# A second Strassen level for three products of the ssm residual, in a conditioned block kernel in float32

## The chip, the cores and the metric

The kernel runs on one core of a Trainium2 chip. The metric is the device time of one execution in microseconds; the median of several runs is given. TensorE (PE in the profile; PEld is its loading of weights) multiplies, VectorE (DVE), ScalarE (ACT) and GpSimd (POOL) work on elements, SyncE (SP) issues most transfers. Each engine takes its instructions in the order in which the program lists them.

## The reference

The reference is one block of a conditioned network over `x` of 2 x 2048 x 512, in float32. With the conditioning row `t` of each of the two batch entries it computes six rows of 512, normalizes, multiplies twice by 512 x 512 weights (the ssm part), and after a second normalization by weights of 512 x 1024 and 1024 x 512 (the ff part). Each part is scaled by a gate and added to `x`:

```python
emb = jnp.dot(jax.nn.silu(t), ada_w) + ada_b
shift_msa, scale_msa, gate_msa, shift_mlp, scale_mlp, gate_mlp = jnp.split(emb, 6, axis=-1)
norm = _ln(x) * (1.0 + scale_msa[:, None]) + shift_msa[:, None]
h = jax.nn.gelu(jnp.dot(norm, ssm_w1) + ssm_b1, approximate=False)
x = x + gate_msa[:, None] * (jnp.dot(h, ssm_w2) + ssm_b2)
norm2 = _ln(x) * (1.0 + scale_mlp[:, None]) + shift_mlp[:, None]
hf = jax.nn.gelu(jnp.dot(norm2, ff_w1) + ff_b1, approximate=True)
x = x + gate_mlp[:, None] * (jnp.dot(hf, ff_w2) + ff_b2)
```

## The kernel before

The 4096 rows are cut into 8 blocks of 512, numbered 0 to 7; blocks 4 to 7 belong to the second batch entry and have other gates. A block passes four stages on TensorE, which the names of the PSUM tiles tell apart: `hA` (hidden of the ssm part), `oA` (residual of the ssm part), `hC` (hidden of the ff part) and `oC` (residual of the ff part). The loop at the end of the kernel interleaves two blocks: with `i` for the block in its ff part, it issues `hC` of block i, `oA` of block i + 1, `oC` of block i and `hA` of block i + 2. Near the end (`ahead`, i = 5) `hA` of block 7 comes before `oC` of block 5, and `oA` of block 7 after it.

Every product is done in Strassen's form. `hA` and `oA` use one level: seven products `P1` to `P7` of half sizes in place of eight, each of eight TensorE records (`group`, the matmul at L475). The operand sums that Strassen needs are made on GpSimd or VectorE (`cut_sum`, L348). `hC` uses a fixed program of 26 products (`products`, L985) whose operand sums `forms` are listed in `HK_B` (20 sums, L923) and whose results are read at L999 (ScalarE) and L1002 (VectorE). `oC` (`residual_in_leaves`) does `P1` and `P6` plainly (L778) and the other five products by a second level: seven rounds, in each of which one leaf of every one of the five products is multiplied (L824), 128 columns wide.

What TensorE sums up in PSUM is added to `x` by VectorE: L739 in `oA`, L789, L838 and L874 in `oC`. In `oA` the result of P1 is not read alone: ScalarE copies it into another bank (L489), on which P2 is added.

PSUM is handed out from two pools: `ps_t` with two banks of the tag `t`, and `ps_g` with two banks for each of the tags `y`, `x` and `v`. A new tile takes the bank of the tile before the last one of its tag, and its first write waits until that tile has been read. The bias rows, already multiplied by the gates, are written into the banks ahead of time (`seed`, L447 and L445).

The order of the work around the matmuls is written out by hand: `hooks` maps a place (a product or a round) to the operations that are issued behind it. So an operation of VectorE that is hooked behind a round stands in VectorE's queue between the reads of that round and the reads of the next.

A normalization (`Norm`) has these steps: `stats` on VectorE (L512, L513); `scales`, eight small instructions on 128 x 4 elements, one of them a power, on GpSimd (L548 to L566); `normal` on ScalarE (L580); `turn`, a transpose in 32 x 32 pieces on VectorE (L591); `move`, 16 transfers that finish the transpose (L600); and `modulate` on ScalarE (L623). Then come the sums for `hA` (`summed`) or the 20 `forms` for `hC`.

The second weights of both parts are multiplied by the gate of the batch entry (`weight_of_second`, L396). This is done again when block 4 begins: `w2` is loaded anew in `oC` of block 2 and multiplied in `hA` of block 4, with the gate row taken into PSUM by `take_gate` (L336); `fw2` follows in `hA` of block 5.

Of the kernel before, what the change touches and what calls it, by code (L numbers as in the profile page):

```python
# [140 lines left out]
def kernel(  # L141
# [97 lines left out]
    ident = const.tile([P, P], F32, tag="ident", name="ident")  # L239
# [20 lines left out]
    b2_bc = work.tile([P, D], F32, tag="gb", name="gb2_0", bufs=2)  # L260
# [39 lines left out]
    def gate_rows_of(g, tag):  # L300
        pa = rows_of(g)
        r = work.tile([P, P] if g == 2 else [P, D], F32, tag=tag, name=f"grows_{g}", bufs=1)
        nc.vector.tensor_tensor(r[:, :P], pa[:, :P], gate_b[g], ALU.add)
        gate_rows[g] = r
# [16 lines left out]
    def store_gates(g):  # L321

        to = gates_dram[g].rearrange("b (n m q) -> m b n q", n=KD, q=G)
        for m in range(P // G):
            rows_m = gate_rows[g][m * G : m * G + B, :P].rearrange("p (n q) -> p n q", n=KD)
            nc.sync.dma_start(out=to[m], in_=rows_m)

    def load_gate(g, b):

        t = work.tile([P, D], F32, tag="g5", name=f"gsb_{g}_{b}", bufs=1)  # L330
        gate_rows[g, b] = load_row(t, gates_dram[g][b])
# [59 lines left out]
    def weight_of_second(w_sb, s, gt, engs, cut=1):  # L391
# [15 lines left out]
        return second_operands(q, s), ops + sums_of_second(q, s, nc.gpsimd, cut)  # L407
# [22 lines left out]

    Q = P // C
# [17 lines left out]
    leaf_row = const.tile([P, 3, P], F32, tag="leaf_row", name="leaf_row")  # L449
    nc.gpsimd.memset(leaf_row, 0.0)  # L450

    def apart_leaves(row, eng):
        a, b = slice(D // 2, D // 2 + P), slice(D // 2 + P, D)
        eng.tensor_tensor(leaf_row[:, 2], row[:, b], row[:, a], ALU.subtract)
# [44 lines left out]
    class Norm:  # L499
# [30 lines left out]
        def squares_on_act(self):  # L530
# [9 lines left out]
            return [lambda: nc.gpsimd.tensor_scalar(less, self.mv[:, :, 0], -1.0, None, ALU.mult)] + [  # L540
# [3 lines left out]
        def scales(self, on_dve=False):  # L544

            n, v = self.name, nc.gpsimd
            ve = small.tile([P, C], F32, tag="ve", name=f"ve{n}")
            v.tensor_scalar(ve, self.mv[:, :, 1], self.of_squares, EPS, ALU.mult, ALU.add)  # L548
            r = small.tile([P, C], F32, tag="r", name=f"r{n}")
            v.tensor_tensor(r, ve, minus_half, ALU.pow)  # L550
            e = small.tile([P, C], F32, tag="e", name=f"e{n}")
            self.rstd = small.tile([P, C], F32, tag="rstd", name=f"rstd{n}")
            self.nmr = small.tile([P, C], F32, tag="nmr", name=f"nmr{n}")
            if on_dve:
                v = nc.vector
                v.tensor_tensor(e, r, ve, ALU.mult)
                v.scalar_tensor_tensor(e, e, -0.5, r, ALU.mult, ALU.mult)
                v.scalar_tensor_tensor(self.rstd, e, 1.5, r, ALU.add, ALU.mult)
                v.scalar_tensor_tensor(self.nmr, self.mv[:, :, 0], -1.0, self.rstd, ALU.mult, ALU.mult)
                return  # L560
            v.tensor_tensor(e, r, r, ALU.mult)
# [4 lines left out]
            v.tensor_scalar(self.nmr, self.nmr, -1.0, None, ALU.mult)  # L566

# [70 lines left out]
        def registers(self):  # L638
# [4 lines left out]
            ]  # L643

# [110 lines left out]

    LEAVES = ("P1", "P2", "P6", "P5", "P7", "P3", "P4")
# [4 lines left out]
    def residual_in_leaves(name, i, hops, wops, leaf_wops, kdim, hooks, last, five, carried):  # L761
# [36 lines left out]
        }  # L798
        seeded = ps["v"].rearrange("p j d -> p (j d)").rearrange("p (n d) -> p n d", d=P)
# [6 lines left out]
        if five:  # L806
            nc.scalar.copy(rooms["P4", "v"][:, :3, :], leaf_row)
# [90 lines left out]
    def gate_bias(g, b, row, name):  # L898

        t = load_row(work.tile([P, D], F32, tag="gb", name=name, bufs=2), row)  # L900
# [14 lines left out]
    def sums_of_registers(program, reg, engs):  # L915


        def op(n, d, f, a, b):
            eng = engs[n % len(engs)]
            if f == "n":  # L920
# [6 lines left out]
    class First:  # L927
# [8 lines left out]
        def summed(self, eng):  # L936
# [3 lines left out]
            return sums_of_first(q, s, eng)  # L940

# [3 lines left out]
    class Second:  # L945
# [77 lines left out]
        def leaf_sums(self, nxt, nx2, five, engs):  # L1023
# [7 lines left out]
            else:  # L1031
                flat = forms.rearrange("p n a r -> p (n a r)")
                r24, r35 = flat[:, : 6 * W], flat[:, 6 * W : (6 + 3 * n35) * W]
                r7 = [flat[:, (12 + n) * W : (13 + n) * W] for n in range(3)]
# [30 lines left out]
    silu = const.tile([P, KD, G], F32, tag="silu", name="silu")  # L1065
# [43 lines left out]
    n1[0].scales(on_dve=True)  # L1109
# [37 lines left out]
    hook(hooks, ("P2",), [lambda: gate_rows_of(2, "grows")] + n1_sums[3:])  # L1147
# [23 lines left out]
    def ff_gate():  # L1171
        take_gate(5, 0)
        found["fw2"] = weight_of_second(fw2_sb, fw2_s, gate[5, 0], (nc.vector,), 4)
# [4 lines left out]
    def gb5_0():  # L1178
        nc.gpsimd.tensor_tensor(gb[5], gate_rows[5, 0], gb[5], ALU.mult)
# [9 lines left out]
    hook(hooks, ("P6",), [lambda: gate_rows_of(5, "g5")])  # L1189
    hook(hooks, ("P6", "P6", "P7", "P7"), [lambda c=c: n2[0].turn(c) for c in range(C)])  # L1190
    hook(hooks, ("P7",), [lambda: n2[0].move((nc.sync,), (0, 1)), lambda: store_gates(5), lambda: load_gate(5, 0)])
    fb2_bc = work.tile([P, D], F32, tag="gb", name="gb5_0", bufs=2)
    load_row(fb2_bc, fb2)
    load_x(2)
    gb[5] = fb2_bc
# [26 lines left out]
    hook(hooks, ("P2",), [n1[2].move, gb5_0])  # L1222
# [3 lines left out]
    hook(hooks, ("P4",), [lambda: store_gates(2)])  # L1226
# [33 lines left out]
    hook(hooks, ("P1",) * 3 + ("P2", "P2", "P6", "P6", "P5", "P5", "P7", "P3"), take(11))  # L1260
# [15 lines left out]

    later, unread_stats = [], []
    for i in range(1, NBLK):
# [7 lines left out]
        if i == 1:  # L1286
# [4 lines left out]
            hook(hooks, (0,), [n1[i + 2].scales])  # L1291
        elif unread_stats:
            hook(hooks, (1, 2, 3, 5, 7), unread_stats)
        if nx2:
            hook(hooks, (3,), [lambda: load_x(i + 1)])
            hook(hooks, (3, 3, 4, 4) if ahead else (1, 2, 3, 4), hA[i + 1].summed(nc.gpsimd))
        elif nxt:
# [196 lines left out]
```

## Time and profile before

| | |
|---|---|
| time, median of 3 runs | 586.76 us (586.58 to 587.15) |
| profiled execution, span | 584.7 us |
| lies around the span, in the median | 2.06 us |
| PE busy | 577.8 us, 99% |
| DVE busy | 416.3 us, 71% |
| POOL busy | 428.2 us, 73% |
| ACT busy | 263.2 us, 45% |

The span runs from the first instruction to the last of one profiled execution. The execution's own time has no record besides its span; the median of the runs shown lies 2.06 us above it. In the rows of a timeline the columns are the start in us, the time taken in us, the engine, the line, the operation, what is written and read, the shapes and the count; in brackets the idle time of the engine ahead of it and what ended it. In the chain the columns are the start, the time and the group of instructions.

### The profile page before, as it was taken

To read this page: it belongs to the slowest core of one execution; us is meant where nothing else is said; L and a number is where in the kernel's file an instruction comes from. 1 tells how busy PE (TensorE), PEld (TensorE's weight loads), DVE (VectorE), ACT (ScalarE), POOL (GpSimd) and SP (SyncE) were. 2 spreads that over 40 slices of the span, in tenths; PEclk is the share of its full clock that TensorE was granted. 3 is DMA by queue.
4 is the path that set the end of the run, shared out by engine and by line. 5 is a ranking of instruction groups with operands and counts; after the bars stand their busy time and mean duration, and the time that the engine had idled before them with its cause. 6 is when DMAs were issued, how large, how long until landed. Compare 5 with 4: busy or idle time off the path is not lost.

```text
span 584.7 us, 9487 instructions
## 1 busy us (share of the span) xinstructions
PE 577.8 (99%) x3303; PEld 515.5 (88%) x3303; DVE 416.3 (71%) x752; ACT 263.2 (45%) x479; POOL 428.2 (73%) x518
## 2 busy tenths in 40 slices
PE   8999999999999999999999999999999999999997
PEld 4888888888889888998889988898888998899896
DVE  4978788987968375685756856884756367787676
ACT  2234357405642555435742588226673331731420
POOL 2875359999997938969788799998679445369351
PEclk9999999999999999999999999999999999999999
DMA  8990322303205403372043820244130330031002
GB/s 317 396 394 11 91 64 79 112 36 108 56 19 166 142 1 72 107 218 73 2 91 71 290 73 22 52 84 154 52 73 0 112 107 1 1 73 72 2 1 72
DMA packets 25243, 56.49 MB, mean 97 GB/s; under 512 B 4672, under 2 KB 5740, under 8 KB 23532
## 3 DMA queue, kind: packets, MB, share of 16 engines
q1 hardware_dynamic: 21856, 51.67, 27.9%
q10 hardware_dynamic: 3340, 4.22, 2.9%
q8 instruction: 26, 0.43, 0.3%
q14 instruction: 21, 0.17, 0.1%
HBM read 32.80 MB, written 8.40 MB: 70 GB/s over the span
## 4 chain that ended last, share of the span: by engine, by line
PE 93%; DMA 3%; DVE 2%; issue 0%; DVEq 0%
PE px_hC L985 10%; PE py_oA L475 9%; PE py_hA L475 9%; PE py_hC L985 8%; PE py_oC L778 8%; PE pv_hC L985 8%; PE pl_oC_P_y L824 8%; PE pv_oA L475 5%; PE pl_oC_P_v L824 5%; PE pv_hA L475 4%; PE pl_oC_P_x L824 3%; PE py_oC L475 2%; PE py_hC L475 2%; PE px_oA L475 2%; DMA ada<-in_L_cond_ada_w_dram 2%; PE px_hA L475 2%
## 5 line engine op out<-in xcount | busy, mean ns | idle before, releaser
L348 POOL TENSOR_TENSOR hSC<-hClo,hChi 128x512 f32<-128x512 f32 (+1 forms) x16 | 19.7, 1236 | 39.6 <-ACT hChi L980 34.2
L623 ACT ACTIVATE nT<-nT,mod,mod 128x512 f32<-128x512 f32 x32 | 23.4, 803 | 55.4 <-DMA nT<-blocks 39.8
L512 DVE BATCH_NORM_STATS2 st<-x 128x6 f32<-128x512 f32 x60 | 40.6, 678 | 5.4 <-DMA x<-in_x_dram 5.1
L923 POOL TENSOR_TENSOR forms<-forms 128x256 f32<-128x256 f32 x56 | 41.8, 747 | 3.3
L985 PE MATMUL py_hC<-forms,fw 128*128 128x256 f32 x168 | 41.0, 380 | 0.0
L1002 DVE TENSOR_TENSOR hClo<-hClo,py_hC 128x512 f32<-128x512 f32 x42 | 28.6, 684 | 15.3 <-ACT hClo L999 9.4
L985 PEld LDWEIGHTS py_hC<-forms,fw 128*128 128x128 f32 x168 | 31.7, 190 | 4.7 <-ACT hChi L999 0.2
L591 DVE STREAM_TRANSPOSE blocks<-nT 128x512 f32<-128x512 f32 x32 | 22.2, 705 | 13.5 <-ACT nT L580 13.5
L923 POOL TENSOR_TENSOR forms<-nT,forms 128x256 f32<-128x256 f32 x42 | 30.5, 748 | 1.7 <-PE pl_oC_P_v L824 1.3
L623 ACT ACTIVATE x<-x,mod,mod 128x512 f32<-128x512 f32 x24 | 17.6, 802 | 31.6 <-DMA x<-blocks 31.6
L923 POOL TENSOR_TENSOR forms<-nT 128x256 f32<-128x256 f32 x14 | 10.4, 741 | 28.4 <-ACT nT L623 18.0
L1002 DVE TENSOR_TENSOR hChi<-hChi,pv_hC 128x512 f32<-128x512 f32 x35 | 23.3, 681 | 10.4 <-PE pv_hC L985 6.7
L580 ACT ACTIVATE nT<-x,nmr,rstd 128x512 f32<-128x512 f32 x32 | 24.1, 806 | 13.3 <-POOL nmr L566 13.3
L985 PE MATMUL px_hC<-forms,fw 128*128 128x256 f32 x112 | 27.6, 379 | 0.0
L980 ACT ACTIVATE hClo<-hClo,colsT 128x256 f32<-128x256 f32 x56 | 25.3, 500 | 5.0 <-DVE hClo L1002 4.8
L838 DVE TENSOR_TENSOR x<-pl_oC_P_y,x 128x256 f32<-128x256 f32 (+1 forms) x66 | 24.7, 375 | 3.0 <-PE pl_oC_P_y L824 1.2
L475 PE MATMUL py_oA<-w,hA 128*128 128x256 f32 x112 | 26.5, 379 | 0.0
L999 ACT ACTIVATE hChi<-py_hC 128x512 f32<-128x512 f32 x14 | 7.6, 593 | 41.2 <-PE py_hC L985 41.0
L980 ACT ACTIVATE hChi<-hChi,colsT 128x256 f32<-128x256 f32 x56 | 25.1, 497 | 1.9 <-DVE hChi L1002 1.9
L739 DVE TENSOR_TENSOR x<-py_oA,x 128x512 f32<-128x512 f32 x26 | 17.8, 686 | 11.2 <-PE py_oA L475 10.6
L778 PE MATMUL py_oC<-fw_s,hSC 128*128 128x256 f32 x112 | 25.3, 379 | 0.0
L778 PE MATMUL py_oC<-fw,hClo 128*128 128x256 f32 x112 | 25.3, 379 | 0.0
(339 smaller groups left out, 1781.1 us busy)
## 6 DMA issues: line engine op xcount, KB each, us to landing
x<-in_x_dram SPq DMA_DIRECT2D x13, 1024.0 KB
out_dram<-x SPq DMA_DIRECT2D x14, 512.0 KB
ada<-in_L_cond_ada_w_dram SPq DMA_DIRECT2D x6, 1024.0 KB
x<-blocks SPq DMA_DIRECT2D x96, 64.0 KB
nT<-blocks SPq DMA_DIRECT2D x80, 64.0 KB
fw<-in_L_cond_ff_w_dram SPq DMA_DIRECT2D x2, 2048.0 KB
w<-in_L_cond_ssm_w_dram SPq DMA_DIRECT2D x3, 1024.0 KB
nT<-blocks ACTq DMA_DIRECT2D x48, 64.0 KB
```

What stands on the lines that cost most here:

```text
L475: nc.tensor.matmul(ps[b][j * apart][:, j, :], lhs(p, j, k), rhs(p, j, k), start=(fresh and j * (not apart) == 0 and k == 0), stop=(p in (" ...
L512: nc.vector.bn_stats(st, xs[self.i][:, c, :])
L580: nc.scalar.activation(t, x_c, AF.Identity, bias=self.nmr[:, c : c + 1], scale=self.rstd[:, c : c + 1])
L591: nc.vector.transpose(self.bl[:, :, :, c, :].rearrange("p m k q -> p k m q"), self.nT[:, c, :].rearrange("p (k m q) -> p k m q", k=KD, m=C),)
L623: nc.scalar.activation(dst, src, AF.Identity, bias=shift, scale=scale)
L778: yield lambda j=j, k=k: nc.tensor.matmul(ps[BANK[p]][:, j, :], hops(p, j, k), wops[p][:, k, :], start=False, stop=(k == kdim - 1), skip_g ...
L824: nc.tensor.matmul(t[:, n, :], hops.leaves[p][f][:, k, :], leaf_wops[p][f][:, k, :], start=room not in started, stop=(f in ("P2", "P3", "P ...
L838: nc.vector.tensor_tensor(d, src, d, ALU.add)
L923: eng.tensor_tensor(reg[d], reg[a], reg[b], ALU.add if f == "+" else ALU.subtract)
L980: nc.scalar.activation(h, h, AF.Gelu_apprx_tanh, bias=fb1T[:, m : m + 1])
L985: nc.tensor.matmul(ps[b][:, j, :], fa[ra][:, j * P : (j + 1) * P], fb[rb].rearrange("p a (c q) -> p c a q", q=Q), start=(fresh and j == 0) ...
L1002: nc.vector.tensor_tensor(dest(d), dest(d), ps[b], op)
```

## The change

In `oA` of blocks 3 to 6 the products P2, P3 and P4 are done by a second Strassen level, in a new function. P1, P5, P6 and P7 stay as they were. Three leaves are multiplied in each of seven rounds `R0` to `R6`, which alternate with the plain products; the result of each round is read by VectorE in two pieces. The leaves need sums of `h` (`leaf_sums` of `First`, eight on GpSimd per block, in `hC`) and of `w2` (`leaves_of_w2`, eight on GpSimd for each of the two gates); `plain_w2` takes back the part of these that is done in place, ahead of block 7.

The small steps of the normalization are split into `root` (VectorE and the power on GpSimd) and `steps` or `rest` (VectorE, with intermediate results in PSUM); the normalizations 1 and 2 of the first blocks (`early`) keep them on GpSimd. Six of the 20 `forms` go from GpSimd to VectorE in most blocks (`beside`); ScalarE copies one operand of each into PSUM first. The sums of the ff leaves get another order on GpSimd. The new multiplication of `w2` by the gate goes into `oC` of block 2 and reads the gate row from SBUF. Loads of gate and bias rows get other places and tiles of their own.

```diff
+    STEPS = ("P1", "R0", "P5", "R1", "R2", "P6", "R3", "R4", "P7", "R5", "R6")
+    STEP_OF = {"P1": "P1", "P2": "P5", "P6": "P6", "P5": "R4", "P7": "P7", "P3": "R5", "P4": "R6"}
+
+    def residual_with_leaves(name, i, hops, wops, leaf_wops, hooks):
...
+        plain_dests = {"P1": x_1[:, 0, :, :1], "P5": x_1[:, :, :, 1].rearrange("p h t f -> p t h f"), "P6": x_1[:, 0, :, 1:], "P7": x_1[:, 1]}
...
+            d = plain_dests[p]
+            nc.vector.tensor_tensor(d, ps[BANK[p]].unsqueeze(2).to_broadcast(d.shape), d, ALU.add)
+
+        def leaf_round(r):
+            f = LEAVES[r]
+            b = LEAF_BANK[f]
+            for n, p in enumerate(("P2", "P3", "P4")):
+                nc.tensor.matmul(
+                    rooms[b][:, n, :],
+                    hops.leaves[p][f],
+                    leaf_wops[p][f],
...
+            if r == 0:
+                nc.scalar.copy(rooms["x"][:, :3], rooms["y"][:, :3])
...
+            for d, n in ((X[:, 0, t, :, e, :], slice(0, 2)), (X[:, 1, t, :1, e, :], slice(2, 3))):
+                nc.vector.tensor_tensor(d, rooms[b][:, n], d, ALU.add)
...
+            v = nc.gpsimd if self.early else nc.vector
...
+            v.tensor_scalar(self.ve, self.mv[:, :, 1], self.of_squares, EPS, ALU.mult, ALU.add)
+            nc.gpsimd.tensor_tensor(self.r, self.ve, minus_half, ALU.pow)
...
+            return [
+                begin,
+                lambda: v.tensor_tensor(parts[1], self.r, parts[0], ALU.mult),
+                lambda: v.scalar_tensor_tensor(parts[1], parts[1], -0.5, self.r, ALU.mult, ALU.mult),
+                lambda: v.scalar_tensor_tensor(parts[2], parts[1], 1.5, self.r, ALU.add, ALU.mult),
+                lambda: v.scalar_tensor_tensor(self.rstd, parts[1], 1.5, self.r, ALU.add, ALU.mult),
+                lambda: v.scalar_tensor_tensor(self.nmr, self.mv[:, :, 0], -1.0, parts[2], ALU.mult, ALU.mult),
+            ]
...
+            if d in beside:
+                ra, rb = (copied[a], reg[b]) if a in copied else (reg[a], copied[b])
+                nc.vector.tensor_tensor(reg[d], ra, rb, ALU.add if f == "+" else ALU.subtract)
...
+            if i > 1:
+                hook(hooks, (10,), hA[i + 1].leaf_sums(nc.gpsimd))
+            hook(hooks, (10,), late_sums)
...
-            hook(hooks, ("P5",), sums24)
-        if fold:
-            sums35 = sums35[:2] + sums7[:2] + sums35[2:] + sums7[2:]
-        elif nx2:
-            hook(hooks, ("P7",), sums7)
+            hook(hooks, ("P5",), sums24[:2])
         if nx2:
+            thirds_fourths = [s[n] for n in (2, 3) for s in (sums24, sums35, sums7)]
+            sums35 = sums35[:2] + sums7[:2] + thirds_fourths
...
-            residual(f"oA_{i + 1}", i + 1, hA[i + 1], w2_ops, KD // 2, hooks, order=CARRIED)
+            if i == 1:
+                residual(f"oA_{i + 1}", i + 1, hA[i + 1], w2_ops, KD // 2, hooks, order=CARRIED)
+            else:
+                residual_with_leaves(f"oA_{i + 1}", i + 1, hA[i + 1], w2_ops, w2_leaf, hooks)
...
-            if leaf_fold:
-                hook(hooks, ("P1",), leaf_fold[:2])
-            hook(hooks, ("P1",), [lambda: n2[i + 1].scales()])
+            hook(hooks, ("P1",), [lambda: n2[i + 1].root()])
+            hook(hooks, ("P1",), (leaf_fold or [])[:-2] + [lambda: n2[i + 1].rest(found["room"])])
             hook(hooks, ("P1",), sums35)
...
-                hook(hooks, ("P1",), leaf_fold[2:])
+                hook(hooks, ("P5", "P7"), leaf_fold[-2:])
...
             hook(hooks, ("P1",), [lambda: load_w("w2", w2, w2_sb)])
+            w2_ops, w2_fold = weight_of_second(w2_sb, w2_s, gate_rows[2, b], (nc.vector,))
+            hook(hooks, ("R2", "R4", "R4", "P3"), w2_fold[:KD])
...
-            run(form((nc.gpsimd,)))
+            begin = lambda: run(form((nc.gpsimd,), () if refold5 else (19, 17, 12, 11, 2, 7)))
...
+        hook(hooks, ("P1",), [begin])
...
-            take_gate(2, b)
-            w2_ops, w2_fold = weight_of_second(w2_sb, w2_s, gate[2, b], (nc.vector,))
-            hook(hooks, ALL, [multiply_2] + w2_fold)
...
+            hook(hooks, ("P4",), w2_fold[KD:])
...
+            plain_w2(w2_sb, w2_s, nc.vector)
             residual(f"oA_{i + 2}", i + 2, hA[i + 2], w2_ops, KD // 2, hooks, order=CARRIED)
```

In the ff residual, the place `R2` lies behind round 3, and `R4` and `P3` lie behind round 5.

More of the change, by code (lines that the diff above doesn't have):

```diff
@@ L566, in scales, with steps, begin @@
             v.tensor_scalar(self.nmr, self.nmr, -1.0, None, ALU.mult)
+        def steps(self, scratch=None):
+            n, v, parts = self.name, nc.vector, []
+            def begin():
+                self.rstd, self.nmr = [small.tile([P, C], F32, tag=t, name=f"{t}{n}") for t in ("rstd", "nmr")]
+                room = scratch
+                if room is None:
+                    room = ps_t.tile([P, D], F32, tag="t", name=f"small{n}")
+                parts.extend([room[:, j * C : (j + 1) * C] for j in range(3)])
+                v.tensor_scalar(parts[0], self.mv[:, :, 1], self.of_squares, EPS, ALU.mult, ALU.add)
+            return [
[6 more added lines that the diff above has]
+            ]
         def blocks(self):
@@ L1274 @@
     fold = None
+    late_sums = []
     later, unread_stats = [], []
```

207 lines of the change are left out of this document (147 added, 60 removed).

## The prediction

> **What bounds the kernel now.** I read the page first (span, engine busy times, slices, chain), then the chain in order of time, then each engine's timeline around block 3's ssm residual, then the windows by stage.
>
> ```profile
> span 584.7 us, 9487 instructions
> PE 577.8 (99%) x3303; PEld 515.5 (88%) x3303; DVE 416.3 (71%) x752; ACT 263.2 (45%) x479; POOL 428.2 (73%) x518
> PEclk9999999999999999999999999999999999999999
> PE 93%; DMA 3%; DVE 2%; issue 0%; DVEq 0%
> 188.72 1.73 PE py_hA L475 x8
> 223.26 1.73 PE py_oA L475 x8
> 233.62 1.73 PE py_oA L475 x8
> 235.35 3.45 PE py_oC L778 x16
> 244.49 2.23 PE pl_oC_P_x L824 x20
> 257.88 1.73 PE py_hA L475 x8
> 259.61 1.73 PE pv_hA L475 x8
> 327.05 1.73 PE py_hA L475 x8
> 396.46 1.73 PE py_hA L475 x8
> ```
>
> The reader is to see that TensorE is the bound without a gap. One block takes 257.88 - 188.72 = 69.16 us and the next 327.05 - 257.88 = 69.17. The one after takes 69.41, so about 0.25 us of waiting in a whole block. The clock is at its top all along. So only two things can move the time: fewer TensorE cycles, or a new wait on TensorE. No speeding up of another engine can gain by itself. The profiled execution gives 584.7 us of span; the runs shown have a median of 586.76. I take the 2.06 us between them as fixed, work out the change of the span, and add it to 586.76. About 0.2% of the time, 1.2 us, is what a measurement of this kernel can tell from no change.
>
> **What TensorE saves.** The ssm residual of block 3 runs from 223.26 to 235.35: 12.09 us, seven products of 1.727 us, each 8 records of 256 columns. A leaf round of the ff residual is 20 records of 128 columns in 2.23 us, 0.1115 each, although each pair needs weights of its own; so their loading is covered at that width. After the change four products stay (6.91 us) and seven rounds of three leaves come, 42 records: 4.68 us. The stage takes 11.59 us in place of 12.09: 0.50 saved. Blocks 3 to 6 together: 2.0 us. This is the whole gain there can be, bar the 0.25 above: a floor of 584.5 to 584.8.
>
> **What VectorE is given.**
>
> ```profile
> 226.92 0.69 DVE L739 TENSOR_TENSOR x<-pv_oA,x 128x512 f32<-128x512 f32 x1 [2.93 <-ACT pv_oC L445]
> 250.18 1.22 DVE L874 TENSOR_TENSOR x<-py_oC,x 128x1024 f32<-128x1024 f32 x1
> 255.69 1.08 DVE L838 TENSOR_TENSOR x<-pl_oC_P_v,x 128x256 f32<-128x256 f32 x3 [0.92 <-PE pl_oC_P_v L824]
> 257.20 0.42 DVE L838 TENSOR_TENSOR x<-pv_oC,x 128x256 f32<-128x256 f32 x1
> 257.92 0.75 DVE L838 TENSOR_TENSOR x<-pl_oC_P_y,x 128x128 f32<-128x128 f32 x2 [0.29 <-PE pl_oC_P_y L824]
> 223.30:235.40 12.10, 12.10 (x57) 10.64 (x56) 5.04 (x10) 4.61 (x11) 10.24 (x9) 1.00 0.42 102
> 235.40:257.90 22.50, 22.50 (x173) 21.70 (x172) 16.04 (x36) 9.57 (x16) 16.55 (x23) 1.00 0.50 145
> 361.80:373.90 12.10, 12.10 (x58) 10.65 (x57) 8.38 (x13) 4.43 (x11) 11.94 (x11) 1.00 0.39 89
> ```
>
> (The windows give span, then the busy time of PE, PEld, DVE, ACT and POOL.) Now the residual's reads are six of 0.69: 4.1 us. After it P1 and P6 take 0.69 each, P5 and P7 go to two quarters and take 1.22 each, and six rounds take 0.42 + 0.375 each: 8.6 us, 4.4 more. In blocks 3 and 4 VectorE had 5.04 us of work in this stage, so 9.5 of 11.6 fits. TensorE comes back to a bank soonest at P7, which adds to the bank that P6's read must leave: two rounds (1.34 us) lie between, the read needs 0.69 and the 0.2 that a read starts behind its matmul, so 0.4 is spare. No wait there. In block 5 the stage already had 8.38 us, since four sums of ff weights are hooked into it, and 12.8 does not fit into 11.6: VectorE enters the ff residual behind it, block 4's, 1.2 us late.
>
> The normalization's small steps go from GpSimd to VectorE. Block 3's rows, and one such step as VectorE does it at the start of the kernel:
>
> ```profile
> 238.85 1.04 POOL L550 TENSOR_TENSOR r<-ve,minus_half 128x4 f32<-128x4 f32 x1
> 241.36 0.23 POOL L566 TENSOR_SCALAR nmr<-nmr 128x4 f32<-128x4 f32 x1
> 10.19 0.16 DVE L558 SCALAR_TENSOR_TENSOR rstd<-e,r 128x4 f32<-128x4 f32 x1
> 217.86 1.27 POOL L348 TENSOR_TENSOR hSC<-hClo,hChi 128x512 f32<-128x512 f32 x1 [8.59 <-ACT hChi L980]
> 250.41 1.27 POOL L348 TENSOR_TENSOR nS<-x,nS 128x512 f32<-128x512 f32 x1
> 256.14 0.73 POOL L923 TENSOR_TENSOR forms<-nT 128x256 f32<-128x256 f32 x1 [4.46 <-DMA x<-in_x_dram]
> ```
>
> About seven steps of 0.16 to 0.2 on VectorE (1.3 us) replace seven on GpSimd. The power stays on GpSimd, 1.04 us, and VectorE waits for it with the reads of the ff residual queued behind; these come only after 9 us of that stage, so this costs nothing. `nmr` comes about 1 us later than now (241.36 + 0.23). Its followers (normal, turn, move, modulate, forms) end in forms that start at 256.14; the next ff product, which reads them, begins seven products after 257.88, at 269.97, or 0.5 earlier: covered by more than 10 us. GpSimd gets eight leaf sums per block (four as 128x256, 0.7 each, four half of it: 4.3 us) and in two blocks as much again for w2. They go into the 8.59 us in which it stood idle before 217.86: nothing on the path. The six forms on VectorE cost two copies on ScalarE and six reads of 0.42 in a stage where VectorE has room: nothing.
>
> **The wait I expect first.** In block 2's ff residual, which stands behind block 3's ssm residual, four multiplications of w2 by the gate are now hooked on VectorE, one after round 3 and three between the reads of round 5 and those of round 6. Behind them is queued the read of `pv_oC` (257.20, ended 257.62). It frees the bank in which P5 of block 4's hidden product (ssm) starts at 259.61: 2.0 us spare now.
>
> ```profile
> 260.06 1.87 DVE L396 TENSOR_TENSOR w<-w,pgate 128x512 f32<-128x512 f32 x3
> 332.54 0.97 DVE L348 TENSOR_TENSOR fw_t<-fw 128x512 f32<-128x512 f32 x1
> 333.54 1.09 DVE L348 TENSOR_TENSOR fw_t<-fw,fw_t 128x512 f32<-128x512 f32 x1
> 366.10 1.32 DVE L348 TENSOR_TENSOR fw<-fw 128x512 f32<-128x512 f32 x1
> 365.60 1.27 POOL L348 TENSOR_TENSOR hClo<-hClo 128x512 f32<-128x512 f32 x1
> 366.83 1.72 POOL L348 TENSOR_TENSOR hSC<-hChi,hSC 128x512 f32<-128x512 f32 x1
> ```
>
> Round 5's reads end at 255.69 + 1.08 = 256.77. The two reads up to `pv_oC` need 0.34 + 0.42. So 259.61 - 256.77 - 0.76 = 2.08 us are left for three multiplications. Before, the gate lay in PSUM and three took 1.87: they would fit, wait 0. Now the gate lies in SBUF. VectorE's sums with both operands in SBUF took 0.97, 1.09 and 1.32 beside a working GpSimd, and the last pair of rows shows how: the add issued at 366.10 ends 0.55 after GpSimd's sum of 365.60, and GpSimd's next takes 1.72 in place of 1.27. GpSimd will be at work: sums of the ff leaves (two of 1.27, four of 0.73) move behind the normalization, so its `nS` sums, done at 250.41 + 1.27 now, end near 256.5, when the forms begin. With 1.32 + 0.97 + 1.09 = 3.4 the wait is 1.3 us, once. I take that, since these rows are the same shape beside the same neighbour; the bounds are 0 and 2.0 (three of 1.32 are 4.0, less 2.08).
> The Trainium skill speaks against this edit: by its page "SBUF — State Buffer", section "Who interferes with whom", a VectorE instruction with two SBUF inputs and a GpSimd one that reads SBUF exclude each other for a whole instruction. An estimate by that rule: 3 x 0.62 plus 1.27 + 0.73 + 0.73 waited for is 4.6, a wait of 2.5. The 366 rows agree with it; 0.97 and 1.09 show less than a whole instruction waited. What that mechanism gives by rows alone is the last rival below.
>
> **The second wait, in block 4's ff residual.**
>
> ```profile
> 382.20 2.93 ACT L580 ACTIVATE nT<-x,nmr,rstd 128x512 f32<-128x512 f32 x4 [1.92 <-POOL nmr L566]
> 383.05 2.83 DVE L591 STREAM_TRANSPOSE blocks<-nT 128x512 f32<-128x512 f32 x4 [2.09 <-ACT nT L580]
> 390.86 1.59 DVE L838 TENSOR_TENSOR x<-pl_oC_P_v,x 128x256 f32<-128x256 f32 x4
> 392.00 2.23 PE pl_oC_P_v L824 x20
> ```
>
> Here VectorE enters late (1.2), then has four weight sums, then the small steps, then the turns and the reads in one unbroken row; one more weight sum (0.42) is put ahead of round 3's reads. Round 5 (392.00) writes the bank that the first of round 3's reads left at about 391.28: 0.7 spare. Of the 1.2 + 0.42 late, 0.9 is over; against it `nmr` no longer queues behind GpSimd's sums. I take 0.8 us, bounds 0 and 1.6 (the small steps' 1.3 added in part).
>
> **The rest.**
>
> ```profile
> 8.21 0.20 POOL L548 TENSOR_SCALAR ve<-mv 128x4 f32<-128x4 f32 x1 [6.12 <-DVE mv L513]
> 8.44 0.42 DVE L1106 COPY fw_t<-ident 128x512 f32<-128x512 f32 x1
> 13.02 1.97 PE L609 MATMUL pt<-ident,blocks 128*128 128x128 f32 x16
> ```
>
> Each is bounded from both sides. The first block's `ve` moves behind VectorE's copy, from 8.21 to 8.86, and one step more makes `nmr` 0.9 us later; normal then ends near 13.0, when the transposes begin (13.02) behind TensorE's own modulation matmuls (0 to 0.4); the sums of block 7's normalized input reach its P7 with nothing spare (0 to 0.5); in block 4's ff product, VectorE's step waits for ScalarE's squares (-0.25 to 0.4, for the 0.25 there may also go). I take 0.5 together, bounds -0.25 and 1.3. The moved gate and bias loads stand on SP ahead of nothing that is due within several us: nothing.
>
> Sum: -2.0 + 1.3 + 0.8 + 0.5 = +0.6 us: **587.4 us**, within 0.2%.
>
> **Rivals.** *The covers hold* (0.25): the three multiplications fall into gaps of GpSimd and cost 0.62 each, and block 4's reads catch up, as VectorE idles 3 to 7 us in each such stage now. Then waits are 0 to 0.8, say 0.4: 586.76 - 2.0 + 0.4 = 585.2. For it: TensorE never waits now, on the same kinds of reads. Against: GpSimd's row has no gap there. *VectorE's SBUF adds decide* (0.32): one mechanism, VectorE and GpSimd taking turns, at its upper end in both places, 2.0 + 1.6, with 0.7 elsewhere: 4.3 - 2.0 = +2.3, 589.1. It makes the kernel slower from 3.2 us of waits on. For it: the 366 rows. Against: 332 and 333. *The leaves don't run at 0.11 us* is excluded by the 20 records in 2.23.
>
> **How the numbers follow.** Forecast 587.4 (0.43), covers hold 585.2 (0.25), turns 589.1 (0.32). The cases lie in the three classes one by one: faster 0.25, same 0.43, slower 0.32. The range reaches from 584.9, just over the floor, to 589.2; what is left out is waits of nothing at all and those over 4.4 us, 1 in 10 each. The forecast's own range is 585.6 to 587.9.
>
> **What would show it.** Right: the chain shows 1.73 x4 and seven short rounds, 11.6 us, in blocks 3 to 6; P5 of block 4's hidden product starts about 1.3 us behind P1's end; rounds 4 and 5 of block 4's ff residual are stretched; the blocks' periods become 68.7 where nothing waits. Wrong: w2's multiplications at 0.62 to 0.7 each, or a gap of TensorE over 0.5 us in a place not named here, above all at a bank's first matmul behind P6 or R2.

## Result: slower by 0.42%, and the profile after

| | before | after |
|---|---|---|
| time, median | 586.51 us (586.39 to 587.15, 9 runs) | 589.06 us (587.60 to 591.45, 9 runs) |
| ratio | | 1.0042 [1.0030, 1.0054] |
| span of the profiled execution | 584.7 us | 587.5 us |

The times after also scatter over 3.9 us, those before over 0.8. The page of the kernel after:

```profile
span 587.5 us, 9787 instructions
PE 578.7 (99%) x3375; PEld 516.2 (88%) x3375; DVE 449.9 (77%) x899; ACT 268.2 (46%) x495; POOL 421.8 (72%) x462
PEclk9999999999999999999999999999999999999999
PE 89%; DVE 6%; DMA 2%; issue 1%; ACT 0%; POOL 0%; DVEq 0%; POOLq 0%; ACTq 0%
```

The clock is the same. VectorE has 34 us more work and GpSimd 6 less, as the change says. The chain (last line) is the first sign of what happened: the share that was not TensorE's was 3% DMA and 2% DVE before; now DVE has 6%. The chain in order of time shows block 3's ssm residual, and two transfers that stand in the chain in the middle of the run:

```profile
224.56 1.73 PE py_oA L832 x8
226.29 0.67 PE pl_oA_y L847 x6
...
235.49 0.67 PE pl_oA_y L847 x6
236.16 0.86 PE py_oC L897 x4
...
268.33 4.12 DMA gb<-in_L_cond_ssm_b_dram
...
325.21 8.23 DMA fw<-in_L_cond_ff_w_dram
333.54 2.48 DVE fw L397 x4
```

The residual runs from 224.56 to 236.16, 11.6 us with short rounds of 0.67: the leaves do what was forecast. To find the loss, the two traces were cut into stages, from the first matmul of a stage to the first of the next. All stages that are not in this table have the same length in both within 0.1 us, except the start, which is 0.28 us shorter after (the first matmul 0.16 earlier, the first hidden stage 0.12 shorter). The columns behind `after` are the experiments told below; each is one profiled execution.

| stage, us | before | after | e1 | e2 | e8 | e3 | e4 | e6 | e7 | e9 | e10 | e11 | e12 |
|---|---|---|---|---|---|---|---|---|---|---|---|---|---|
| hC, block 1 | 22.45 | 23.63 | 23.64 | 22.46 | 22.59 | 23.68 | 23.65 | 23.62 | 22.46 | 22.45 | 22.48 | 22.45 | 22.47 |
| oC, block 1 | 22.54 | 22.85 | 22.84 | 22.84 | 22.86 | 22.84 | 22.83 | 22.84 | 22.84 | 22.86 | 22.54 | 22.54 | 22.54 |
| oA, blocks 3, 4, 6, each | 12.09 | 11.59 | 11.59 | 11.59 | 11.59 | 11.59 | 11.59 | 12.09 | 11.59 | 12.09 | 11.59 | 11.59 | 11.59 |
| hA, block 4 | 12.09 | 12.09 | 12.09 | 12.09 | 12.09 | 12.09 | 12.09 | 12.09 | 12.09 | 12.09 | 12.09 | 12.09 | 12.09 |
| hC, block 3 | 22.45 | 23.83 | 23.82 | 23.85 | 23.83 | 22.48 | 23.81 | 24.60 | 22.50 | 22.50 | 22.52 | 22.48 | 22.50 |
| hA, block 5 | 12.09 | 13.90 | 12.09 | 13.24 | 12.26 | 12.09 | 12.09 | 12.09 | 12.09 | 12.09 | 12.09 | 12.09 | 12.09 |
| hC, block 4 | 22.70 | 22.65 | 22.50 | 22.75 | 22.65 | 22.50 | 22.60 | 22.50 | 22.56 | 22.56 | 22.57 | 22.56 | 24.04 |
| oA, block 5 | 12.09 | 11.76 | 11.92 | 11.59 | 11.89 | 12.09 | 11.59 | 12.09 | 11.59 | 12.09 | 12.03 | 12.23 | 11.59 |
| oC, block 4 | 22.54 | 22.54 | 22.57 | 22.54 | 22.60 | 22.58 | 22.90 | 22.54 | 22.92 | 22.54 | 24.62 | 22.58 | 22.54 |
| hC, block 6 | 22.45 | 22.59 | 22.59 | 22.59 | 22.59 | 22.59 | 22.59 | 22.59 | 22.59 | 22.59 | 22.59 | 22.59 | 22.60 |
| span | 584.7 | 587.5 | 586.4 | 586.1 | 585.0 | 584.9 | 585.8 | 588.6 | 584.4 | 584.9 | 585.2 | 583.3 | 584.1 |
| time, median | 586.51 | 589.06 | 588.21 | 587.26 | 587.48 | 586.72 | 587.69 | 590.37 | 585.48 | 587.48 | 586.89 | 584.94 | 586.27 |

The four residuals gain 0.50 x 3 + 0.33 = 1.83 us. Three stages lose 1.18 (hC of block 1), 1.38 (hC of block 3) and 1.81 (hA of block 5), 4.37 together; oC of block 1 loses 0.31 and hC of block 6 0.14. With the start's -0.28 and smaller ones this is +2.7, against 2.8 between the spans. None of the three is a stage that the prediction named. Each has its own row:

VectorE and GpSimd in hC of block 1, before:

```profile
135.67 0.42 DVE L923 TENSOR_TENSOR fw<-fw 128x256 f32<-128x256 f32 x1
137.54 1.27 POOL L348 TENSOR_TENSOR hSA<-hA 128x512 f32<-128x512 f32 x1
```

The same after:

```profile
135.90 1.52 DVE L1047 TENSOR_TENSOR fw<-fw 128x256 f32<-128x256 f32 x1
137.35 0.68 DVE L1140 TENSOR_TENSOR hChi<-hChi,px_hC 128x512 f32<-128x512 f32 x1
135.87 1.27 POOL L349 TENSOR_TENSOR hSA<-hA 128x512 f32<-128x512 f32 x1
138.07 2.11 PE L1123 MATMUL px_hC<-forms,fw_s 128*128 128x256 f32 x7 [0.58 <-DVE hChi L1140]
```

A weight sum of 0.42 us takes 1.52; the read behind it begins 1.35 later than before (137.35, 136.00 before), and TensorE waits for it. What differs is GpSimd: `hSA` now begins with the weight sum, not 1.9 us behind it.

VectorE, and TensorE's first wait, in hC of block 3, after:

```profile
272.55 0.69 DVE L1023 TENSOR_TENSOR gb<-pgate,gb 128x512 f32<-128x512 f32 x1 [1.88 <-DMA gb<-in_L_cond_ssm_b_dram]
273.28 0.55 DVE L478 TENSOR_TENSOR gb<-gb 128x256 f32<-128x256 f32 x1
274.57 1.27 DVE L1140 TENSOR_TENSOR hChi<-hChi,pv_hC 128x512 f32<-128x512 f32 x2
277.49 1.13 PE L1123 MATMUL px_hC<-forms,fw_s 128*128 128x256 f32 x4 [0.66 <-ACT hClo L1137]
```

VectorE stands 1.88 us at the bias multiplication because its row has not landed, and the first reads of the stage (274.57, 3.95 into the stage, which began at 270.62) queue behind; the last row is a matmul that waits further on. Before, these reads stood 2.03 into the stage and waited for TensorE:

```profile
271.84 1.29 DVE L1002 TENSOR_TENSOR hChi<-hChi,pv_hC 128x512 f32<-128x512 f32 x2 [0.88 <-PE pv_hC L985]
```

Without the 1.88 us they would have stood at 2.07.

Who waited in hA of block 5, before, and then after (engine and line, what it waited for, us, times, longest):

```profile
DVE fw L396 <- DMA fw<-in_L_cond_ff_w_dram: 0.8, 1, 0.8
```

```profile
DVE fw L397 <- DMA fw<-in_L_cond_ff_w_dram: 4.0, 1, 4.0
...
PE py_hA L495 <- DVE hA L757: 1.6, 1, 1.6
```

Here the first multiplication of the reloaded fw2 waits for its transfer, and the read L757, on which TensorE's P4 waits, is queued behind seven of these multiplications and two sums.

### The profile page after: what moved, and what is told of

Read it like the earlier page. It is cut to its first block, busy times and chain, and to the rows that moved or that the text cites. A ratio compares the mean times of both kernels' runs of the same rounds, so it can differ in the third digit from the quotient of the medians.

```text
span 587.5 us, 9787 instructions
## 1 busy us (share of the span) xinstructions
PE 578.7 (99%) x3375; PEld 516.2 (88%) x3375; DVE 449.9 (77%) x899; ACT 268.2 (46%) x495; POOL 421.8 (72%) x462
## 4 chain that ended last, share of the span: by engine, by line
PE 89%; DVE 6%; DMA 2%; issue 1%; ACT 0%; POOL 0%; DVEq 0%; POOLq 0%; ACTq 0%
PE px_hC L1123 9%; PE py_oC L897 8%; PE py_hA L495 8%; PE pv_hC L1123 8%; PE py_hC L1123 7%; PE pl_oC_P_y L945 7%; PE py_oA L495 5%; PE pl_oC_P_v L945 4%; PE pv_hA L495 4%; PE py_oA L832 4%; PE pl_oC_P_x L945 3%; PE py_hC L495 2%; PE pv_oA L495 2%; PE px_hA L495 2%; PE pl_oA_y L847 2%; PE pv_oC L945 2%
## 5 line engine op out<-in xcount | busy, mean ns | idle before, releaser
L575 POOL TENSOR_TENSOR r<-ve,minus_half 128x4 f32<-128x4 f32 x16 | 16.6, 1036 | 62.0 <-DVE ve L574 20.0
L1137 ACT ACTIVATE hClo<-px_hC 128x512 f32<-128x512 f32 x21 | 12.5, 596 | 30.6 <-PE px_hC L1123 20.2
L349 POOL TENSOR_TENSOR hClo<-hClo 128x512 f32<-128x512 f32 (+1 forms) x23 | 24.5, 1070 | 0.0
L1123 PEld LDWEIGHTS px_hC<-forms,fw 128*128 128x128 f32 x112 | 21.3, 190 | 2.9
```

The source lines that it names most:

```text
L349: eng.tensor_tensor(out[:, r], a[:, r], b[:, r], f)
L1123: nc.tensor.matmul(ps[b][:, j, :], fa[ra][:, j * P : (j + 1) * P], fb[rb].rearrange("p a (c q) -> p c a q", q=Q), start=(fresh and j == 0) ...
```

## The experiments

All start from the kernel after. A first set takes one loss each; e10 to e12 build on e7.

**e1, GpSimd's sums hooked later.**

```diff
-hook(hooks, (3, 3, 4, 4) if ahead else (1, 2, 3, 4), hA[i + 1].summed(nc.gpsimd))
+hook(hooks, (3, 3, 4, 4) if ahead else (3, 4, 5, 6) if i == 1 else (1, 2, 3, 4), hA[i + 1].summed(nc.gpsimd))
```

> The four sums of block 2's ssm hidden rows (hSA, hA; GpSimd) are hooked two products later in block 1's ff hidden stage; nothing else differs from the changed kernel, in whose trace this stage is 23.63 us in place of 22.46. Theory A (the small steps that left GpSimd let its sums begin 1.67 us earlier, beside VectorE's weight sum fw<-fw, both operands in SBUF, which then takes 1.52 in place of 0.42): the weight sum takes about 0.4 again, the gap of 0.74 us at product 7 goes, the stage takes 22.5 us, the time falls by 1.1. Rival B (VectorE itself has too much in this stage, its new small steps first of all): the stage stays at 23.4 to 23.7 and the time at that of the changed kernel. The two other losses (3rd ff hidden stage +1.4, block 5's ssm hidden stage +1.8) stay where they are under both.

Measured: 588.21 us (ratio 1.0030 [1.0021, 1.0040]), the stage 23.64. By its words this went to rival B, but the rows show that the edit did not make the difference that it was meant to make:

```profile
136.62 1.27 POOL L349 TENSOR_TENSOR hSA<-hA 128x512 f32<-128x512 f32 x1
136.65 1.52 DVE L1047 TENSOR_TENSOR fw<-fw 128x256 f32<-128x256 f32 x1
```

A hook sets an order in GpSimd's queue, not a time. Nothing stood ahead of `hSA` and it waited for nothing, so it still began right behind the power. The run is inconclusive for A and B; e8 was made for that. Its other finding is hA of block 5: 12.09, although nothing there was touched.

**e2, the small steps of this stage on GpSimd again.** For block 3's first normalization alone `early` is true, and `rest` stands at product 0 in place of the six `steps`.

> The small steps of block 3's first normalization, which fall into block 1's ff hidden stage, go back to GpSimd as they were before; nothing else differs from the changed kernel. The stage took 23.63 us there, and 23.64 with the sums hooked two products later, which left them where they were on GpSimd, right behind the power. Theory A (the small steps had kept GpSimd off VectorE's weight sum): the sums begin 1.7 us later again, the weight sum takes 0.4 in place of 1.52, and the stage 22.5. Rival B (VectorE has too much in this stage): also 22.5, since six small steps leave it; so this run checks the size alone, and the next one tells them apart.

Measured: the stage 22.46, the weight sum 0.41, time 587.26 (ratio 1.0022 [1.0008, 1.0036]).

**e8, six idle steps on GpSimd.**

```diff
 hook(hooks, (0,), [n1[i + 2].root])
+spare = small.tile([P, C], F32, tag="spare", name="spare", bufs=1)
+hook(hooks, (0,), [lambda: nc.gpsimd.tensor_scalar(spare, minus_half, -1.0, None, ALU.mult)] * 6)
 hook(hooks, (7, 8, 9, 10, 11, 11), n1[i + 2].steps())
```

> Nothing of the changed kernel is moved or taken out; six idle small instructions on GpSimd (128 x 4, written to a tile that nobody reads) are put behind the power in block 1's ff hidden stage, where the normalization's small steps had been. VectorE keeps all of its work. Theory A (what the small steps did there was to hold GpSimd's sums back while VectorE makes its weight sum): more work on GpSimd makes the stage shorter, 22.5 us in place of 23.63, the weight sum takes 0.4. Rival B (VectorE's own work is too much there): the stage stays at 23.6 or more.

Measured: the stage 22.59, time 587.48 (ratio 1.0018 [1.0008, 1.0029]). VectorE and GpSimd:

```profile
135.94 0.45 DVE L1047 TENSOR_TENSOR fw<-fw 128x256 f32<-128x256 f32 x1
135.92 1.75 POOL L1430 TENSOR_SCALAR spare<-minus_half 128x4 f32<-128x4 f32 x6
137.64 1.27 POOL L349 TENSOR_TENSOR hSA<-hA 128x512 f32<-128x512 f32 x1
```

Six instructions that compute nothing take 1.04 of the 1.18 us away, with VectorE's work unchanged. This decides it: the small steps had been holding GpSimd's long sums off VectorE's weight sum. Taking them from GpSimd took that away.

**e3, the bias multiplication later.**

```diff
-hook(hooks, ("P5", "P4"), [lambda: found.update(gb2=bias_2()), lambda: found["gb2"]()])
+hook(hooks, ("P5",), [lambda: found.update(gb2=bias_2())])
 ...
+if i == 3:
+    hook(hooks, (6,), [lambda: found["gb2"]()])
```

> The multiplication of the second bias row b2 by the gate (two VectorE instructions) moves from P4 of block 4's ssm hidden product to behind product 6 of block 3's ff hidden stage; nothing else differs from the changed kernel, where that stage takes 23.84 us in place of 22.45. Theory A (VectorE stands 1.9 us at the multiplication until the row's transfer, issued at 268.33, has landed, and the reads of the stage's first products queue behind it): without the wait the stage takes 22.4 to 22.6 us, the time falls by 1.3. Rival B (the stage is late because of the normalization's statistics and small steps on VectorE, or because of w2's sums on GpSimd): the stage keeps 23.5 us or more. The other two losses stay.

Measured: 586.72 us (586.11 to 587.41; ratio 1.0004 [0.9995, 1.0013]), the stage 22.48. Its VectorE rows:

```profile
272.99 1.28 DVE L1140 TENSOR_TENSOR hChi<-hChi,pv_hC 128x512 f32<-128x512 f32 x2 [1.15 <-PE pv_hC L1123]
274.19 0.96 DVE L574 TENSOR_SCALAR ve<-mv 128x4 f32<-128x4 f32 x1
...
278.92 1.29 DVE L478 TENSOR_TENSOR gb<-gb 128x256 f32<-128x256 f32 x1
```

VectorE waits for TensorE again, not the other way round, and the multiplication's second part costs nothing there though it now takes 1.29. Theory A holds, with one limit: the run moves the two instructions together with the wait, so it does not part the 1.88 us of waiting from their 1.24 us of work. The reckoning above does: less the wait alone, the reads would have stood where they did before. The time fell by 2.3, more than the 1.3 expected. hA of block 5 was at 12.09 in its profile too.

**e4, fw2 ahead of x.**

```diff
-hook(hooks, ("P5",), [lambda: load_x(i + 3)])
+if i != 3:
+    hook(hooks, ("P5",), [lambda: load_x(i + 3)])
 ...
 load_half("fw2", fw2, fw2_sb, 0)
+load_x(i + 3)
 store(i, 0)
```

> The transfer of block 6's x (1 MB) is issued behind the two halves of fw2 in place of ahead of them; nothing else differs from the changed kernel, where block 5's ssm hidden stage takes 13.90 us in place of 12.09 and VectorE stands 4.0 us at the first multiplication of fw2 until its transfer has landed. Theory A (the landing decides: fw2 queues behind x): the multiplication begins 1.5 to 2.5 us earlier by the stage's start, the stage takes 12.1 to 12.3 us and the time falls by 1.6 to 1.8. Rival B (the new order of VectorE's and GpSimd's work there decides: forms begun behind P1, the bias multiplication at P4, the sums of the ff leaves): the stage keeps 13.5 us or more. Rival C (the late landing was an accident of one execution): the stage is short here, and also in kernels that leave the order of the transfers alone.

Measured: 587.69 us (587.34 to 588.39; ratio 1.0024 [1.0014, 1.0033]), the stage 12.09. The time fell by 1.4, the span of the profile by 1.7 (oC of block 4 lost 0.36). Here A and C are both right in part. The start of the first fw2 multiplication, counted from the start of hA of block 5, and the stage's loss, in all profiles:

| | before | after | e2 | e8 | e3 | e6 | e1 | e4, e7, e9 to e12 (fw2 first) |
|---|---|---|---|---|---|---|---|---|
| begins at, us | +3.26 | +4.95 | +4.21 | +3.67 | +2.54 | +2.16 | +2.10 | +1.72 to +2.06 |
| stage over 12.09 | 0 | 1.81 | 1.15 | 0.17 | 0 | 0 | 0 | 0 |

The stage loses where the first multiplication begins later than some point between +3.3 and +3.7, and the more the later. With the old order of the transfers the start differs by 2.9 us between kernels that leave the transfers here alone. So the 1.81 is no fixed price; it is what a late landing cost in that execution, and the kernel before, with 0.8 us of wait and no loss, stood next to it. With fw2 ahead of x the landing is early in all six profiles, and the times of e4, e7, e9 and e10 scatter over 1.1 us each in place of after's 3.9 (e11 and e12 are as narrow but for one or two runs). But e3, in the old order, scatters over 1.3 only, so the order is not the whole reason. Why the landing is late is not settled. fw2 is issued 3.38 us ahead of the stage in every profile. x, which is ahead of it in the old order, is issued 5.2 to 5.4 ahead of the stage in after, e2 and e8, 5.8 and 5.9 in e3 and e1, and 6.9 in e6: where x is issued later, fw2 is mostly later too. But the kernel before, with x at 6.1, is later than e1 and e3, and no run moved x's issue alone.

**e6, without the leaves.** `residual` in place of `residual_with_leaves`, no leaf sums, no `plain_w2`. In this run block 7's first modulation, hooked at a round that the plain product lacks, was left out as well.

> The leaves alone are taken back: the ssm residual of blocks 3 to 6 is plain, and the leaf sums of h and w2 on GpSimd and the step that takes them back are left out; all else is as in the changed kernel. Theory A (the leaves save 0.50 us in each of four stages, the losses come from the supporting moves): the four stages take 12.09 us again, the losses in the three hidden stages (1.2, 1.4, 1.8) stay, and the time is 2 us above the changed kernel, 590.5 to 591. Rival B (the losses come from the leaves' own sums on GpSimd and reads on VectorE): the three losses go, and the time is about that of the kernel before, 586.5 to 587.

Measured: 590.37 us (ratio 1.0065 [1.0046, 1.0084], 4 runs); with a part of the work left out, the time is a rough one. The residuals are at 12.09 again and the losses of the two ff hidden stages stay. That of block 3 grows to 2.15: the second of the two bias instructions (L478) takes 1.51 us there, beside a GpSimd sum, in place of 0.55. For these two stages rival B falls: their losses come from the supporting moves. hA of block 5 is at 12.09 here, which theory A did not expect, so this run says nothing of that loss.

**e7 and e9, the three repairs (e2, e3, e4) with and without the leaves.** In e9 the modulation left out in e6 is in its place.

> Three repairs at once, with all the leaves kept: block 3's first small steps on GpSimd, the bias multiplication behind product 6, fw2's transfer ahead of x's. If the three losses are the whole account, the four ssm residual stages keep their 11.6 us (block 5's up to 12.1) and all else is as before: span 583.0 to 583.6, time 584.8 to 585.4, faster than the kernel before by 0.2 to 0.3%. If repairing them only moves the waits on, the time is 586 or more.

> The same three repairs, but the ssm residual of blocks 3 to 6 plain and without leaf sums: what the supporting moves are worth without the leaves. If the leaves are worth their TensorE records and no more, this kernel is 1.5 to 2.0 us slower than the one with the three repairs and the leaves, and within 0.5 us of the kernel before. If the leaves cost something elsewhere (reads on VectorE, sums on GpSimd), the difference is 1 us or less.

Measured: e7 585.48 us (585.05 to 586.20; ratio 0.9982 [0.9973, 0.9990]); e9 587.48 (586.98 to 588.08; ratio 1.0015 [1.0006, 1.0024]). e7's time is 0.1 above the range expected. By the medians the leaves are worth 587.48 - 585.48 = 2.0 us, what their matmul records say, but that it fits so closely is partly chance. The four residuals differ by 1.99 between the two profiles, of which oC of block 4 takes 0.38 back, and the medians of the spans differ by 1.7 (583.7 and 585.4). The other 0.3 lies outside the spans: an execution's time is 2.08 above its span in e9 and 1.80 in e7 (1.79 in the kernel before, 2.04 in e6, which has no leaves either); why is open. The same 0.3 is a part of what puts e9 1.0 us above the kernel before and not within 0.5. Of the other 0.7 the profile shows 0.32 in oC of block 1 and 0.14 in hC of block 6; the rest stays open. The span of e7's profile came out above the range expected because its first matmul was 1.1 us later than in after (15.77 against 14.66; only e1 and e6, at 15.43 and 15.20, are late as well).

**e10, the last weight sums of the ff leaves back behind P1.**

```diff
-hook(hooks, ("P1",), (leaf_fold or [])[:-2] + [lambda: n2[i + 1].rest(found["room"])])
+hook(hooks, ("P1",), (leaf_fold or []) + [lambda: n2[i + 1].rest(found["room"])])
 ...
-if leaf_fold:
-    hook(hooks, ("P5", "P7"), leaf_fold[-2:])
```

> As the kernel with the three repairs and the leaves, but the last two weight sums of the ff leaves stand behind P1 of the ff residual of blocks 1 and 4, where they were before, in place of P5 and P7. In the kernel with the three repairs these stages take 22.84 and 22.92 us against 22.54 in all others, and the sum fw<-fw ahead of round 3's reads takes 1.45 us in block 1 (beside a GpSimd sum) and 0.42 in block 4. Theory A (a sum of two SBUF operands put ahead of a round's reads holds up the bank of the next round): both stages take 22.54 us, the time is 584.8. Rival B (VectorE has too much in these stages, wherever the sums stand): the loss appears elsewhere in the same stage, which stays above 22.7.

Measured: 586.89 us (ratio 1.0005 [0.9996, 1.0014]). In block 1 theory A holds, 22.54; in block 4 the stage grows to 24.62, and the time is not theory A's 584.8. VectorE's rows, two of block 1 and two of block 4, and TensorE's wait in block 4:

```profile
171.03 0.42 DVE L349 TENSOR_TENSOR fw<-fw 128x256 f32<-128x256 f32 x1
171.36 0.42 DVE L349 TENSOR_TENSOR fw_t<-fw,fw_t 128x256 f32<-128x256 f32 x1
...
379.15 1.49 DVE L349 TENSOR_TENSOR fw<-fw 128x256 f32<-128x256 f32 x1
380.56 1.49 DVE L349 TENSOR_TENSOR fw_t<-fw,fw_t 128x256 f32<-128x256 f32 x1
```

```profile
PE pl_oC_P_y L945 <- DVE x L959: 1.1, 1, 1.1
```

The same two sums: 0.42 each in block 1, where GpSimd is at its power on 128 x 4 elements (170.41 to 171.54), and 1.49 each in block 4, beside GpSimd's sums of 128 x 512. In block 4 two weight sums more stand ahead of them, and these use up the time of the power. TensorE's 1.1 us is its wait ahead of round 4. The place that is right for one block is wrong for the other.

**e11 and e12.** e11 is e7 with the sums behind P1 in block 1 alone. e12 moves two further sums (128x512) out of block 5's ssm residual, to products 17 and 20 of the hidden stage ahead.

> As the kernel with the three repairs and the leaves, but the last two weight sums of the ff leaves stand behind P1 again in the ff residual of block 1 alone; block 4 keeps them at P5 and P7, since there the move to P1 made that stage 24.62 us long. Theory (each of the two stages by itself: block 1's reads were held up by the 1.45 us sum, block 4's VectorE comes late from an over-full ssm residual stage): block 1's stage 22.54 us, block 4's 22.9, block 5's ssm residual 11.6 to 12.0, time 585.0 to 585.3. Rival: the loss of block 4 grows again with the shift of 0.3 us; time 585.5 or more.

> As the run before, and two of the four fw2 sums that VectorE makes in block 5's ssm residual (128x512 each, 0.7 us) are hooked behind products 17 and 20 of the ff hidden stage ahead of it. Theory A (in block 5's ssm residual VectorE has more work than the 11.6 us hold, and block 4's ff residual pays for it): block 5's ssm residual takes 11.6 us and block 4's ff residual 22.54 to 22.7; the ff hidden stage keeps 22.6; time 584.6 to 585.0. Rival B (the two sums run beside GpSimd's 2.4-us sums there and hold up the reads of the ff hidden stage): that stage loses 0.5 to 2 us, the time is 585.5 to 587.

Measured: e11 584.94 us (584.84 to 586.55; ratio 0.9977 [0.9967, 0.9988]), the fastest of all. oC of block 1 is at 22.54; block 5's residual lost more than expected, 12.23, and oC of block 4 less, 22.58. e12: 586.27 us (ratio 1.0001 [0.9992, 1.0009]); the stages that theory A named and the loss that rival B named both came out. Block 5's residual and block 4's oC are clean (11.59, 22.54), and the hidden stage lost 1.5 us by the sum beside GpSimd's:

```profile
355.07 1.68 DVE L349 TENSOR_TENSOR fw_t<-fw,fw_t 128x512 f32<-128x512 f32 x1
...
353.82 2.39 POOL L349 TENSOR_TENSOR fw_s<-fw,fw_s 128x1024 f32<-128x1024 f32 x1
```

That the residual is clean is no proof of theory A's reason, too much work for VectorE: in e2, e4 and e7 it is at 11.59 with both sums in place. What it hangs on is told below, with the second wait.

## Why the prediction was right or wrong

The likeliest case was no change, at 587.4 us. 589.06 lies above the forecast's own range (585.6 to 587.9), at the upper end of the whole range. Term by term:

**TensorE's saving, -2.0:** right. 0.50 in blocks 3, 4 and 6, and 1.99 in the four residuals between e9 and e7.

**The first wait, +1.3 in hA of block 4:** wrong, 0. The multiplications themselves were sized well: 3.26 against 3.4 forecast. The line of the multiplication by the gate, with the gate in PSUM and in SBUF (nanoseconds, least, median, most):

```profile
L397 DVE TENSOR_TENSOR fw<-fw,pgate x16: 653/676/689, 70.3 to 340.5; 128x512 f32<-128x512 f32 x16
L397 DVE TENSOR_TENSOR w<-w,gsb x4: 682/1102/1211, 253.7 to 259.6; 128x512 f32<-128x512 f32 x4
```

And VectorE's and TensorE's rows at that place:

```profile
256.50 1.08 DVE L959 TENSOR_TENSOR x<-pl_oC_P_v,x 128x256 f32<-128x256 f32 x3 [0.31 <-PE pl_oC_P_v L945]
257.50 3.26 DVE L397 TENSOR_TENSOR w<-w,gsb 128x512 f32<-128x512 f32 x3
261.20 0.42 DVE L959 TENSOR_TENSOR x<-pv_oC,x 128x256 f32<-128x256 f32 x1
260.26 1.89 PE L495 MATMUL pv_hA<-nS,w_s 128*128 128x256 f32 x8
```

P5 begins 0.94 us *ahead* of the read that I said it waits for. The step that failed is "It frees the bank in which P5 of block 4's hidden product (ssm) starts". I had read the bank from the rule of the last tile but one, which does not hold here: in the built program P5 has the bank of `pl_oC_P_v`, the last tile of its tag, whose reads end at 257.58 and stand ahead of the multiplications in VectorE's queue. `pv_oC` has the other bank. A read that ends 2 us ahead of a matmul is no proof that the matmul needs it.

**The second wait, +0.8 around block 4's ff residual:** the place was right, the size and the reason were not. Over their 11.59 and 22.54 the two stages lose together 0 in e2 and e12, 0.17 in after, 0.35 to 0.38 in e1, e8, e4 and e7, 0.54 in e3, 0.68 in e11 and 2.5 in e10. The step that failed is "12.8 does not fit into 11.6": in e2, e4 and e7 the same work fits, at 11.59. What decides in block 5's residual is one weight sum, `fw<-fw` of 128 x 512, whose time depends on what GpSimd does beside it:

| | e4, e7 | e2 | after | e8 | e1 | e10 | e3 | e11 |
|---|---|---|---|---|---|---|---|---|
| the sum takes, us | 0.73 | 0.79 | 1.27 | 1.40 | 1.43 | 1.54 | 1.60 | 1.74 |
| oA of block 5 over 11.59 | 0 | 0 | 0.17 | 0.30 | 0.33 | 0.44 | 0.50 | 0.64 |

Each loss is the time of the sum less 1.10. In e4 and e7, where this sum is short, VectorE comes to the ff residual earlier, and there another one (`fw_t<-fw_s,fw_t`, 128 x 256) takes 1.49 in place of 0.42; the stage loses 0.36 and 0.38, in rounds 4 and 5 as forecast. VectorE's first read in the ff residual comes 0.5 to 0.7 us later into the stage than before, not 1.2, and that alone costs nothing: it does so in e12 too. So this wait also comes from VectorE and GpSimd taking turns, and not from too much work; no run set out to test this, but the rows of all profiles agree.

**The rest, +0.5:** measured about -0.1: the start -0.28, where I gave 0 to 0.4; block 7's hA 0; hC of block 4 -0.05; hC of blocks 0 and 6 +0.08 and +0.14. The 2.06 us around the span set the median of the runs against the span of another execution; taken execution by execution it is 1.8, before and after, so it was rightly held fixed.

**What the sum did not hold.** Two steps that I set at nothing cost the most. "About seven steps of 0.16 to 0.2 on VectorE (1.3 us) replace seven on GpSimd ... so this costs nothing": VectorE's side of it was right. But I asked only what the steps cost where they go, not what happens where they leave: GpSimd's next sum starts 1.7 us earlier, beside a weight sum with both operands in SBUF. The rows for that (366.10 and its neighbours) were quoted further on, for another place. And "The moved gate and bias loads stand on SP ahead of nothing that is due within several us: nothing": I asked what is queued behind the transfer on SP, not which engine waits for its landing. The row is loaded into the tile that holds the gate until the gate has been copied out, and ScalarE's copy of the gate ended at 268.32, so it could not be issued before 268.33; VectorE met its multiplication 1.9 us ahead of the landing, with the stage's reads behind it. The third, fw2's landing in hA of block 5, was next to the edge before (0.8 us waited); the prediction never looked at that margin.

The rival "VectorE's SBUF adds decide" named 589.1, and 589.06 was measured, but that is luck. Its mechanism is at work, with 1.18, 0.31 and 0.17 of the losses; but the first two are in places that it did not name, and in the two that it did name, for 2.0 and 1.6, there are 0 and 0.17. The other 1.38 and 1.81 are landings of transfers. The sign that would show the forecast wrong, "a gap of TensorE over 0.5 us in a place not named here", came three times.

The Trainium skill's page "SBUF — State Buffer", section "Who interferes with whom", says that the one of the two engines that issues second waits for the other's whole instruction. For GpSimd's long sums the runs agree: e12's sum (355.07 + 1.68) ends 0.54 us behind GpSimd's (353.82 + 2.39), and after's (135.90 + 1.52) 0.28 behind `hSA` (135.87 + 1.27), a little less than such sums take alone (0.68 in e7, 0.42). For GpSimd's power they do not: in after, VectorE's sums of 382.30 and 382.64, with their operands in SBUF, take 0.42 each inside a power that runs from 382.14 to 383.26.

## What to carry to other kernels

Work that is taken from an engine has a price at both ends: ask what its queue does with the time, and beside whom. Where one sum can take 0.42 or 1.5 us, a shift of some tenths in one stage moves the loss to another. For every transfer that a change moves, look up who waits for the landing and what is queued behind that wait, and list the margins (a wait of 0.8 us that costs nothing today) as well as the waits. A hook orders a queue; only a dependence or work ahead of it sets a time.

## What the hardware showed that was not expected

Small instructions count too: VectorE's `ve` step on 128 x 4 elements takes 0.16 us alone, and 0.96 in e3's row of 274.19, with one SBUF operand only. The same operation with its result in PSUM (L603) takes 0.154 to 0.163 in all 12 cases of after. The same section of the Trainium skill lists `tensor_scalar` among the operations that can take the port pair shared with GpSimd; the row agrees, though no run here took GpSimd away from it. The reverse held as well: sums with one operand copied to PSUM (L1043) took 0.414 to 0.425 us in all 24 cases.
